# A decoder layer on one core: attention's bias stored four times side by side, and one buffer for the whole-number activations

## The chip, the core and the metric

The program runs on one core of a Trainium2 chip. A core has five engines with a queue of instructions each: TensorE (PE in the profile) multiplies matrices, with weight loads in a row of their own (PEld); VectorE (DVE), ScalarE (ACT) and GpSimd (POOL) work element by element; SyncE (SP) issues DMAs, and ScalarE issues some, too. Each engine takes its instructions in the order of its queue and waits on semaphores for the others. The metric is the device time in microseconds (us) of one execution: 830.32 us is the median of six runs, 827.81 to 832.29.

## The reference, cut to what matters

Input x is (4, 512, 512) in fp32, and a context of (4, 512, 256). Three blocks follow each other, each with a residual and a layer norm behind it:

```python
x = _layernorm(x + attn(x))                # windows of 128 tokens, 16 heads of 16, a table of relative positions
x = _layernorm(x + ssm(ctx_1024, z=x))     # conv, softplus, a scan over 512 steps with 16 states, times silu(x)
x = _layernorm(x + ffn(x))                 # activations quantized to whole numbers, weights by their signs
```

The change touches two places of it. In attention, each window and head has scores of 128 x 128, to which one and the same bias of 128 x 128 is added before the softmax:

```python
scores = jnp.einsum('bwhqd,bwhkd->bwhqk', q, k) * scale
scores = scores + rel_bias[rel]            # rel_bias[rel]: 128 x 128, the same for all heads
```

In the last block the activations are rounded to whole numbers between -128 and 127, with one scale for each token:

```python
s = 127.0 / jnp.max(jnp.abs(x), axis=-1, keepdims=True)
xq = jnp.clip(jnp.round(s * x), -128, 127) / s
```

## The kernel before

**The work.** There are four batches (b = 0 to 3), each of 512 tokens in four windows. For each batch there are these threads of work: `ssm_inputs` (projection, convolution, step sizes), `ssm_steps` (the scan, in 4 quarters q of the channels and 4 groups n of the states), `attn_qk` and four `attn_window` (attention), `ssm_gate` (norm, gate, norm and quantization of the batch), and at the end `ffn` in two halves of 256 tokens a batch, eight halves h in all. `ffn_signs` reads the weights of the last block in the first 200 us, takes their signs on ScalarE (L718) and writes them to DRAM (L719).

**The scan.** For each state tile POOL multiplies du by a broadcast row (L390), ScalarE makes the decay by an exponential (L394), VectorE scans (L396), VectorE or POOL multiplies by a second row (L398, L400), and TensorE sums into y (L404). The two broadcast rows, bc0 and bc1, are loaded by SyncE for each n (L353). The tile of y, times the gate z (L433), is transposed (L436) and added to the residual (L438).

**The bias.** `attn_biases` loads the 128 x 128 bias once and splits it (L539 to L545) into a high part in fp32r, by a cast on ScalarE, and a low part, the rest, by VectorE. The same function splits a row of other biases, whose parts go by DMA into `rows` (L550). In `attn_window`, `scores(g)` takes four heads at a time: a PSUM bank of 128 x 512 gets the bias by two matmuls with the identity (L625), and the queries times the keys on top (L634). That is 4 batches x 4 windows x 4 groups x 2 parts, 128 matmuls. Their moving operand is a view that repeats the 128 columns four times.

**The whole numbers.** In the last part of `ssm_gate`, four tiles t of 128 tokens are scaled and rounded to v (L462), transposed on TensorE (L465), brought back by ScalarE as whole numbers in bf16 to `qT` (L468), and written to DRAM by a DMA that ScalarE issues (L469). `qT` has two buffers. Then the scales of the batch's tokens are transposed (L472), copied to `ir` (L474), and written to DRAM by SyncE (L475). The halves of the last block read both back (L759, L762). There, for each f2 of eight, `gates` multiplies 16 times for g (L778) and VectorE scales (L786), `gated` does the same for u (L802, L811), ScalarE casts the product to a high part hi (L821), POOL takes the rest lo (L823), and `down` multiplies both by the third weights (L830).

**What sets the order.** The threads are woven in Python (`weave`, L885): each has a start time, and what it yields says how far its time advances; this gives every instruction a priority. A planner of the library then places the instructions of each engine one after the other, by priority and by the times of its own model, as soon as their inputs and buffers are free in that model. So a change of a size or of a number of buffers can move instructions that it does not touch. Tiles come from pools; tiles of one tag share its buffers, and a tile that reuses a buffer waits until all readers of the one before, a DMA among them, are done. The tag "part" has two buffers, which xd (L294) and v (L461) share; the tag "state" has four, which the scan's tiles share with the row of biases and its two parts.

Of the kernel before, what the change touches and what calls it, by code (L numbers as in the profile page):

```python
# [10 lines left out]
F32 = mybir.dt.float32  # L11
F32R = mybir.dt.float32r
BF16 = mybir.dt.bfloat16
# [5 lines left out]
P = 128  # L19
# [3 lines left out]
NT = S // P  # L23
NC = H // P
# [38 lines left out]
BP = 2  # L63
# [17 lines left out]
def decoder_layer_kernel(  # L81
# [24 lines left out]
    small = ctx.enter_context(tc.tile_pool(name="small", bufs=4, side="left"))  # L106
# [3 lines left out]
    def bank(name):  # L110
        return psum.tile([P, 512], F32, tag="mm", name=name)

    def ssm_bank(name):
        return psum.tile([P, 512], F32, tag="aux", name=name, bufs=BX)
# [25 lines left out]
    def moments(v, eps, what, home):  # L140

        with tc.high_priority(HP):
            return moments_(v, eps, what, home)
# [37 lines left out]
    def silu(dst, src, back=True):  # L181

        f = nc.scalar.activation(dst, src, AF.Silu)
        if not back:
            return
        with tc.issue_after(f.ins), tc.high_priority(10 * HP):
            nc.scalar.preload_act_table_set("natural_log_exp_and_others")

    def normalize(dst, src, rs, nb, i, func=AF.Identity):
        nc.scalar.activation(dst, src, func, scale=rs[:, i : i + 1], bias=nb[:, i : i + 1])  # L190
# [3 lines left out]
    mp = ctx.enter_context(tc.tile_pool(name="mp", bufs=2, side="right"))  # L194
# [24 lines left out]
    for j in range(NQ):  # L219
# [6 lines left out]
            rhs=col[:, C_AL : C_AL + NE * DS],  # L226
# [188 lines left out]
    def ssm_gate(b):  # L415
        acc = mp.tile([P, NT, DI], F32, tag="acc", name=f"acc{b}", bufs=1)
        for w in range(NT):
            nc.sync.dma_start(out=acc[:, w, :], in_=x0d[b][:, w, :])
        _, rs, nb = moments(acc, 1e-5, f"a{b}", lambda: ssm_bank(f"root_ps{b}"))
        for w in range(NT):  # L420
            normalize(acc[:, w, :], acc[:, w, :], rs, nb, w)

        z = mp.tile([P, NE, S], F32, tag="z", name=f"z{b}", bufs=1)
        silu(z, acc)
        for q in range(NE):
            while f"y{b}{q}" not in done:
                yield 1
            y = ssm_y[b, q]
            if (b, q) in LATE:
                y = mp.tile([P, S], F32, tag="yr", name=f"yr{b}_{q}", bufs=BR)  # L430
                nc.sync.dma_start(out=y, in_=yd[b, q])
            with tc.high_priority(HP):
                nc.vector.tensor_tensor(z[:, q, :], z[:, q, :], y, ALU.mult)  # L433
            pt = ssm_bank(f"yT_ps{b}_{q}")
            for t in range(NT):
                nc.tensor.transpose(pt[:, ts(t, P)], z[:, q, ts(t, P)], ident)  # L436
            to = acc[:, :, ts(q, P)]
            nc.vector.tensor_tensor(to, to, pt.rearrange("p (t e) -> p t e", e=P), ALU.add)  # L438
        yield 4
        mv, rs, nb = moments(acc, 1e-5, f"m{b}", lambda: pt)  # L440
        amax = small.tile([P, NT], F32, tag="amax", name=f"amax{b}", bufs=1)
        for t in range(NT):
            normalize(acc[:, t, :], acc[:, t, :], rs, nb, t)
            nc.vector.tensor_reduce(amax[:, t : t + 1], acc[:, t, :], AX.X, ALU.max, apply_absolute_value=True)
        nc.scalar.dma_start(out=x2d[b], in_=acc)
        yield 4


        s = small.tile([P, NT], F32, tag="s", name=f"s{b}", bufs=1)
        nc.vector.reciprocal(s, amax)  # L450
        nc.vector.tensor_scalar_mul(s, s, 127.0)
        v2 = small.tile([P, NT], F32, tag="v2", name=f"v2{b}", bufs=1)
        nc.gpsimd.tensor_tensor(v2, mv[:, :, 1], rs, ALU.mult)
        nc.gpsimd.tensor_tensor(v2, v2, rs, ALU.mult)
        r2 = rsqrt(v2, 1e-8, NT, f"f{b}")
        iv = inv_s[:, b * NT : (b + 1) * NT]
        nc.gpsimd.tensor_scalar_mul(iv, amax, 1 / 127.0)
        nc.gpsimd.tensor_tensor(iv, iv, r2, ALU.mult)
        yield 4
        for t in range(NT):  # L460
            v = mp.tile([P, H], F32, tag="part", name=f"v{b}_{t}", bufs=BP)  # L461
            nc.scalar.activation(v, acc[:, t, :], AF.Identity, scale=s[:, t : t + 1], bias=consts[ROUND])  # L462
            pt = ssm_bank(f"qT_ps{b}_{t}")
            for c in range(NC):
                nc.tensor.transpose(pt[:, ts(c, P)], v[:, ts(c, P)], ident)  # L465

            qT = mp.tile([P, NC, P], BF16, tag="qT", name=f"qT{b}_{t}", bufs=2)
            nc.scalar.activation(qT.rearrange("p c t -> p (c t)"), pt, AF.Identity, bias=consts[-ROUND])  # L468
            nc.scalar.dma_start(out=qd[b][:, :, ts(t, P)], in_=qT)  # L469
            yield 2  # L470
        pt = ssm_bank(f"is_ps{b}")
        nc.tensor.transpose(pt[:NT, :P], iv, ident)  # L472
        ir = small.tile([NT, P], F32, tag="ir", name=f"ir{b}", bufs=1)
        nc.scalar.copy(ir, pt[:NT, :P])  # L474
        nc.sync.dma_start(out=isd[b], in_=ir)  # L475

# [35 lines left out]
    def attn_biases(aw, ap, aq, ws):  # L512

        ws["v"] = aw.tile([P, NM, NR, NM, 32], F32, tag="wv", name="wv_s")
        ws["d"] = aw.tile([P, NM, H], F32, tag="wd", name="wd_s")
        for c in range(NM):
            for m in range(NM):
                nc.sync.dma_start(
                    out=ws["v"][:, c, :, m, :], in_=wv[ts(c, P), ts(m, P)].rearrange("p (r k) -> p r k", k=32)
                )  # L520
        ws["v"] = ws["v"].rearrange("p c r m k -> p c (r m k)")
        for r in range(NR):
            for m in range(NM):
                c, p0 = divmod((r * NM + m) * 32, P)
                nc.sync.dma_start(out=ws["d"][p0 : p0 + 32, c, :], in_=wd[m * P + r * 32 : m * P + r * 32 + 32, :])
        raw = ap.tile([P, P], F32, tag="at", name="bias")
        nc.sync.dma_start(out=raw, in_=relb)
        row = mp.tile([1, HC + H], F32, tag="state", name="row", bufs=BS)
        for m in range(NM):
            nc.sync.dma_start(  # L530
                out=row[:, :HC].rearrange("o (r m k) -> o m r k", m=NM, k=32)[:, m],
                in_=rows[:, ts(m, P)].rearrange("o (r k) -> o r k", k=32),
            )
        nc.sync.dma_start(out=row[:, HC:], in_=rows[:, HC:])


        def split(v, name, pool, tags):

            bufs = BS if pool is mp else 1  # L539
            hi = pool.tile(list(v.shape), F32R, tag=tags[0], name=f"{name}_hi", bufs=bufs)  # L540
            lo = pool.tile(list(v.shape), F32R, tag=tags[1], name=f"{name}_lo", bufs=bufs)
            with tc.issue_after(ssm_exp[0].ins):
                nc.scalar.copy(hi, v)
            nc.vector.tensor_tensor(lo, v, hi.bitcast(F32), ALU.subtract)
            return hi, lo  # L545

        ws["bias"] = split(raw, "bias", aw, ("bias_hi", "bias_lo"))
        ws["row"] = aw.tile([2, HC + H], F32R, tag="rows", name="rows")
        for i, part in enumerate(split(row, "row", mp, ("state", "state"))):
            nc.sync.dma_start(out=ws["row"][i : i + 1, :].bitcast(F32), in_=part.bitcast(F32))  # L550
        yield 1
# [51 lines left out]
    def attn_window(b, w, aw, ap, aq, ws):  # L603
        n = f"{b}_{w}"
        tok = ts(w, P)
        cT, qT, kT = attn_x[b]
# [15 lines left out]
        def scores(g):  # L622
            psc = bank(f"sc_ps{n}_{g}")
            for i in range(2):
                nc.tensor.matmul(  # L625
                    psc,
                    lhsT=ws["ident"],
                    rhs=ws["bias"][i].unsqueeze(1).to_broadcast([P, 4, P]),
                    start=(i == 0),
                    stop=False,  # L630
                )
            rows_ = ts(g, 32)
            for m in range(NM):
                nc.tensor.matmul(  # L634
                    psc[:, ts(m, 2 * P)],
                    lhsT=qT[rows_, m, tok],
                    rhs=kT[rows_, m, :, tok],
                    start=False,
                    stop=(m == NM - 1),
                    tile_position=(32 * g, 0),  # L640
                )
            nc.vector.tensor_reduce(  # L642
                ntop[:, 4 * g : 4 * g + 4], psc.rearrange("p (h k) -> p h k", k=P), AX.X, ALU.max, negate=True
            )
            pscs[g] = psc

        scores(0)
        yield 1
        pa = None
        for g in range(NG4):  # L650
# [17 lines left out]
            for j in range(4):  # L668
# [3 lines left out]
                    rhs=scT[:, j, :],  # L672
# [324 lines left out]
```

## Time and profile before

| What | Value |
|---|---|
| Median of six runs | 830.32 us (827.81 to 832.29) |
| The profiled execution's own time | 830.23 us |
| Its span, first to last instruction | 828.4 us |
| Mean granted clock of TensorE | 0.956 |
| Busy share PE, DVE, ACT, POOL | 91%, 78%, 71%, 67% |
| L625, high part: count, mean of one | 64, 527 ns |
| L625, low part: count, mean of one | 64, 400 ns |
| L468 (qT): count, mean of one | 16, 679 ns |
| L469 (its DMA): median to landing | 3.0 us |
| L543, cast of the bias, 128 x 128 | 298 ns |
| L544, its low part, 128 x 128 | 281 ns |

The profile is of one execution. Busy time is the time in which an engine executed something. In the slices each digit is the busy share of one fortieth of the span (20.7 us), in tenths. The chain is followed back from the last instruction, at each step to what released it. In lists of instructions in order of time the columns are the start in us, the duration in us, the engine, the line, the operation, the tiles (out<-in, without numbers) and the count; brackets hold the idle time of the engine ahead of it and what ended it. SPq and ACTq are the issue of DMAs from these engines' queues.

### The profile page before, as it was taken

How to read it: one execution, taken by the hardware profiler on the slowest of the kernel's cores; microseconds unless marked ns; L12 is line 12 of the kernel's file. 1: busy time of each engine (PE TensorE's matmuls, PEld its weight loads, DVE VectorE, ACT ScalarE, POOL GpSimd, SP SyncE). 2: the span in 40 equal slices, each digit the busy share in tenths (PEclk: the TensorE clock that was granted, in tenths of full speed). 3: DMA queues.
4: the chain of work that ended last, by engine and by line, in shares of the span. 5: the costliest groups of instructions: out<-in, count | busy, mean ns of one | idle time of the engine just before them, and what ended most of it. 6: DMA issues, size and time to landing. Idle time of an engine off the chain costs nothing.

```text
span 828.4 us, 11702 instructions
## 1 busy us (share of the span) xinstructions
PE 755.2 (91%) x3906; PEld 411.4 (50%) x3906; DVE 649.6 (78%) x943; ACT 590.9 (71%) x1038; POOL 556.6 (67%) x323
## 2 busy tenths in 40 slices
PE   9978899999899999899988998798788999999995
PEld 4323344444344444344434454356464667777773
DVE  5359586898999887989989699979998978453542
ACT  4558789787775976877797877696595777845551
POOL 2157489688678779787865977786989844233342
PEclk9897999999899999999999999989999999999998
DMA  7887789966342437564334285671334112301100
GB/s 213 292 275 215 231 266 323 314 214 216 89 139 100 151 87 262 195 219 150 112 105 131 87 281 198 195 299 47 128 115 139 52 40 102 92 24 51 52 26 26
DMA packets 82784, 129.49 MB, mean 156 GB/s; under 512 B 18690, under 2 KB 29074, under 8 KB 81444
## 3 DMA queue, kind: packets, MB, share of 16 engines
q1 hardware_dynamic: 65844, 108.77, 40.1%
q10 hardware_dynamic: 16880, 19.98, 7.0%
q8 instruction: 31, 0.51, 0.2%
q14 instruction: 29, 0.24, 0.1%
HBM read 91.48 MB, written 37.23 MB: 155 GB/s over the span
## 4 chain that ended last, share of the span: by engine, by line
PE 53%; DVE 21%; ACT 12%; DMA 7%; issue 5%; SPq 1%; POOL 1%; ACTq 0%; DVEq 0%; POOLq 0%
PE d_ps L830 11%; DVE da L396 5%; PE y L404 5%; PE u_ps L802 4%; PE g_ps L778 4%; PE sc_ps L634 4%; DVE state L396 4%; DMA sgd<-sgn_sgd 3%; PE c_ps L568 3%; PE sc_ps L625 2%; PE a_ps L701 2%; ACT da L394 2%; DVE state L398 2%; PE in_ps L273 2%; PE xd_ps L297 2%
## 5 line engine op out<-in xcount | busy, mean ns | idle before, releaser
L390 POOL TENSOR_TENSOR state<-du,bc 128x1024 f32<-128x1024 f32 x128 | 301.7, 2371 | 110.2 <-PE y L404 67.6
L394 ACT ACTIVATE da<-d,a_neg 128x512 f32<-128x512 f32 x256 | 175.1, 697 | 63.4 <-DVE state L398 39.4
L400 POOL TENSOR_TENSOR state<-state,bc 128x1024 f32<-128x1024 f32 x64 | 151.7, 2370 | 38.4 <-DVE state L396 25.0
L396 DVE TENSOR_TENSOR_SCAN state<-da,state 128x512 f32<-128x512 f32 x128 | 152.5, 1208 | 27.7 <-ACT da L394 21.9
L396 DVE TENSOR_TENSOR_SCAN da<-da,state 128x512 f32<-128x512 f32 x128 | 152.9, 1214 | 14.9 <-ACT da L394 14.9
L823 POOL TENSOR_TENSOR lo<-gs,hi 128x512 fp32r<-128x512 f32 x64 | 81.9, 1282 | 107.3 <-ACT hi L821 88.2
L404 PE MATMUL y<-state,sel 128*32 128x512 f32 x512 | 101.5, 641 | 7.6 <-DVE state L398 4.9
L398 DVE TENSOR_TENSOR state<-da,bc 128x512 f32<-128x512 f32 x128 | 84.7, 678 | 0.8
L658 ACT ACTIVATE sc<-sc_ps,ntop 128x128 f32<-128x128 f32 x256 | 73.9, 376 | 12.0 <-DVE ntop L642 11.2
L821 ACT CAST hi<-gs 128x512 fp32r<-128x512 f32 x64 | 39.2, 616 | 59.5 <-DVE gs L811 44.0
L830 PE MATMUL d_ps<-sd,hi 128*128 128x512 f32 x256 | 74.8, 412 | 4.6 <-DVE nb_a L164 2.0
L830 PE MATMUL d_ps<-sd,lo 128*128 128x512 f32 x256 | 76.5, 421 | 0.0
L802 PE MATMUL u_ps<-taken,su 128*128 128x256 bf16 x512 | 67.6, 273 | 8.0 <-DVE gs L811 5.8
L634 PE MATMUL sc_ps<-k,q 32*128 32x256 f32 x256 | 73.8, 411 | 1.0 <-ACT q L590 1.0
L778 PE MATMUL g_ps<-taken,sg 128*128 128x256 bf16 x512 | 68.8, 279 | 4.5 <-DVE gs L811 3.2
L811 DVE TENSOR_TENSOR gs<-gs,u_ps 128x512 f32<-128x512 f32 x64 | 43.4, 680 | 34.9 <-PE u_ps L802 34.9
L786 DVE TENSOR_TENSOR gs<-g_ps,taken 128x512 f32<-128x512 f32 x64 | 43.4, 683 | 33.9 <-PE g_ps L778 30.4
L802 PEld LDWEIGHTS <-su 128*128 128x128 fp8e4 x512 | 46.2, 98 | 32.4 <-issue 24.9
L778 PEld LDWEIGHTS <-sg 128*128 128x128 fp8e4 x512 | 47.5, 100 | 29.1 <-issue 23.0
L634 PEld LDWEIGHTS sc_ps<-k,q 32*128 32x128 f32 x256 | 42.4, 187 | 30.7 <-issue 23.8
L642 DVE TENSOR_REDUCE ntop<-sc_ps 128x4 f32<-128x512 f32 x64 | 43.3, 677 | 14.7 <-PE sc_ps L634 14.5
L830 PEld LDWEIGHTS d_ps<-sd,hi 128*128 128x128 f32 x256 | 45.7, 191 | 17.2 <-DVE nb_a L164 2.8
(161 smaller groups left out, 1185.2 us busy)
## 6 DMA issues: line engine op xcount, KB each, us to landing
d<-dd SPq DMA_DIRECT2D x60, 256.0 KB, 3.9
du<-dud SPq DMA_DIRECT2D x60, 256.0 KB, 4.5
bc<-bcd SPq DMA_DIRECT2D x32, 256.0 KB, 4.1
xT<-in_xT_dram SPq DMA_DIRECT2D x16, 256.0 KB, 4.7
xa<-in_x_dram SPq DMA_DIRECT2D x16, 256.0 KB, 3.5
raw_sgd<-in_wgT_dram SPq DMA_DIRECT2D x16, 256.0 KB, 4.3
ud<-u ACTq DMA_DIRECT2D x4, 1024.0 KB, 4.3
uq<-ud SPq DMA_DIRECT2D x16, 256.0 KB, 2.9
```

What stands on the lines that cost most here:

```text
L390: nc.gpsimd.tensor_tensor(st, du, bb.unsqueeze(1).to_broadcast([P, 2, S]), ALU.mult)
L394: nc.scalar.activation(da, d[:, j, :], AF.Exp, scale=a_neg[:, a : a + 1])
L396: nc.vector.tensor_tensor_scan(to, da, st[:, j, :], 0.0, ALU.mult, ALU.add)
L398: nc.vector.tensor_tensor(st[:, j, :], da, cb, ALU.mult)
L400: nc.gpsimd.tensor_tensor(st, st, cb.unsqueeze(1).to_broadcast([P, 2, S]), ALU.mult)
L404: nc.tensor.matmul(y[ts(j, EB), :], lhsT=sel, rhs=sts[j], start=False, stop=(n == NG - 1), tile_position=(0, EB * j))
L634: nc.tensor.matmul(psc[:, ts(m, 2 * P)], lhsT=qT[rows_, m, tok], rhs=kT[rows_, m, :, tok], start=False, stop=(m == NM - 1), tile_position= ...
L658: nc.scalar.activation(sc[:, j, :], psc[:, ts(j, P)], AF.Exp, bias=ntop[:, h : h + 1])
L778: nc.tensor.matmul(pg[:, ts(j, HS)], lhsT=sg[:, c, ts(2 * f2 + j, P)], rhs=qT[:, c, :], start=(c == 0), stop=(c == NC - 1),)
L802: nc.tensor.matmul(pu[:, ts(j, HS)], lhsT=su[:, c, ts(2 * f2 + j, P)], rhs=qT[:, c, :], start=(c == 0), stop=(c == NC - 1),)
L823: nc.gpsimd.tensor_tensor(lo, g2, hi.bitcast(F32), ALU.subtract)
L830: nc.tensor.matmul(pos[t], lhsT=part[:, j, ts(t, P)], rhs=sd[:, 2 * f2 + j, :], start=(f2 + j == 0 and part is parts[0]), stop=(f2 == NF2 ...
```

## The change

The bias is split from a view that repeats it four times, so its two parts are stored as 128 x 4 x 128, and the matmuls read them as they lie. Each part takes 2 KB in each partition instead of 0.5 KB. The cast and the subtraction are done on 512 columns instead of 128, once. To `qT` the change gives one buffer instead of two (1 KB less in each partition), and `ir` no longer has a buffer of its own: it takes one of the two of the tag "part" (0.5 KB less).

```diff
-            qT = mp.tile([P, NC, P], BF16, tag="qT", name=f"qT{b}_{t}", bufs=2)
+            qT = mp.tile([P, NC, P], BF16, tag="qT", name=f"qT{b}_{t}", bufs=1)
             nc.scalar.activation(qT.rearrange("p c t -> p (c t)"), pt, AF.Identity, bias=consts[-ROUND])
             nc.scalar.dma_start(out=qd[b][:, :, ts(t, P)], in_=qT)
             yield 2
         pt = ssm_bank(f"is_ps{b}")
         nc.tensor.transpose(pt[:NT, :P], iv, ident)
-        ir = small.tile([NT, P], F32, tag="ir", name=f"ir{b}", bufs=1)
+        ir = mp.tile([NT, P], F32, tag="part", name=f"ir{b}", bufs=BP)
...
-        ws["bias"] = split(raw, "bias", aw, ("bias_hi", "bias_lo"))
+
+        ws["bias"] = split(raw.unsqueeze(1).to_broadcast([P, 4, P]), "bias", aw, ("bias_hi", "bias_lo"))
...
                     lhsT=ws["ident"],
-                    rhs=ws["bias"][i].unsqueeze(1).to_broadcast([P, 4, P]),
+                    rhs=ws["bias"][i],
```

The changed kernel has one line more, so that its lines from 546 on are one higher.

## The prediction

> **What bounds the kernel now.** I read the busy rows and the slices of the page first, then a table by stage, then who waits for whom on TensorE.
>
> ```profile
> PE 755.2 (91%) x3906; PEld 411.4 (50%) x3906; DVE 649.6 (78%) x943; ACT 590.9 (71%) x1038; POOL 556.6 (67%) x323
> PE   9978899999899999899988998798788999999995
> PE 53%; DVE 21%; ACT 12%; DMA 7%; issue 5%; SPq 1%; POOL 1%; ACTq 0%; DVEq 0%; POOLq 0%
> ```
>
> TensorE carries the kernel: 91% of the span and 53% of the chain that ended last. The dips in its row lie near the start and between slices 24 and 31. By stage (columns: stretch in us, its length, then busy us with the count of instructions of PE, weight loads, DVE, ACT, POOL, the granted clock, the DMA share and GB/s):
>
> ```profile
> 0.00:60.00 60.00, 52.78 (x115) 21.60 (x117) 27.71 (x47) 29.36 (x46) 17.79 (x25) 0.91 0.81 257
> 560.00:620.00 60.00, 50.75 (x324) 35.18 (x323) 59.39 (x91) 42.29 (x61) 48.72 (x30) 0.97 0.27 93
> 680.00:720.00 40.00, 38.74 (x268) 30.67 (x266) 29.15 (x64) 27.79 (x41) 13.48 (x19) 1.00 0.28 93
> ```
>
> From 560 to 620 VectorE is the bound (59.39 of 60 us) and TensorE waits for it; from 680 on TensorE is the bound. The waits on TensorE between 560 and 640 (us in total, times, longest) say the same, and add up to 12.5 us; from 640 to the end the same view adds up to 2.4 us:
>
> ```profile
> PE u_ps L802 <- DVE gs L811: 3.1, 3, 1.7
> PE y L404 <- DVE state L398: 2.5, 2, 2.4
> PE g_ps L778 <- DVE gs L811: 2.1, 3, 0.9
> PE d_ps L830 <- DVE gs L786: 1.8, 1, 1.8
> ```
>
> So after 640 every microsecond by which TensorE's next input is late lies on the path. The profiled execution took 830.23 us (span 828.4), the median of the runs is 830.32; I sum against 830.23.
>
> **The change part by part.**
>
> *The bias matmuls: 0.* 128 of them read 512 columns, through a view now, side by side then. One pair (start, length):
>
> ```profile
> 256.95 0.50 PE L625 MATMUL sc_ps<-bias_hi,identr 128*128 128x512 f32 x1
> 257.28 0.39 PE L625 MATMUL sc_ps<-bias_lo,identr 128*128 128x512 f32 x1
> 257.51 1.88 PE L273 MATMUL in_ps<-hT,in_s 128*128 128x512 f32 x4
> ```
>
> From the second to the matmul behind it pass 0.23 us. The matmuls of L830 have the same type and width, read contiguous memory, and stand 16 in 3.66 us on the chain (669.63), 0.23 each. The view costs nothing that could be saved. Bounds: 128 x 0.01 us of rounding, -1.3 to 0.
>
> *The split: 0.* bias_hi grows from 0.30 us (the row at 128x128) to about 0.62 (the cast of 128x512 at L821), bias_lo from 0.28 to about 0.68 (the 128x512 tensor op at L398). ScalarE next waits 1.43 us for TensorE (the copy at 35.81), VectorE 2.74 us (the copy at 37.65): both cover it. Without cover, +0.3 and +0.4.
>
> *SyncE's queue: +0.5.* In the built program of the changed kernel the order of queued work is the same on every engine up to the last third, but for the first 60 us: two DMAs (the second weight row bc1 of n=2, and row_lo) stand ahead of the first write of signs, and on ScalarE the two copies of d (L336) come ahead of two exponentials (L394).
>
> ```profile
> 43.34 0.53 SPq L719 DMA_DIRECT2D sgd<-sgn_sgd  x1
> 47.91 1.15 ACT L718 ACTIVATE sgn_sgd<-raw_sgd 128x512 fp8e4<-128x512 f32 x2 [9.55 <-DMA sgd<-sgn_sgd]
> 49.56 0.69 ACT L394 ACTIVATE da<-d,a_neg 128x512 f32<-128x512 f32 x1
> ```
>
> ScalarE stands 9.55 us for that write to land, with the exponentials queued behind and VectorE's scans behind these. Two issues of 0.55 to 0.6 us make it 1.2 late, the swapped copy (0.57) makes the first exponential 1.75 late. But at 53.16 ScalarE waits again (0.97 us) for the third write of signs, which slips only from 49.33 to about 49.8, because the number of DMAs ahead of it is unchanged. Bounds 0 and +1.75; +0.5 is what passes the second wait.
>
> *One qT buffer: +2.5.* Each qT (L468, ScalarE) now waits until the DMA of the one before has landed. Landing:
>
> ```profile
> DMA to landing us min/median/max: 2.2/3.0/5.8
> ```
>
> Batches 0 and 1 keep their order. There only the fourth tile is late: at 370.26 the DMA issued at 364.90 lands at 370.71 (+0.45; the next row on ScalarE waits 0.63 for VectorE), and at 527.89 one lands at 528.59 (+0.7; the next waits 1.59). Covered: 0.
>
> Batch 3 (before: qT at 709.30, 711.17, 714.31, 717.44). A DMA issues some 0.1 us after the instruction ahead of it on ScalarE has started (710.01 against 709.88). The new order is qT0, v2, table load, silu, table load, DMA0, hi2_0_0, qT1, v3, DMA1, hi2_0_1, nt_o, qT2, root, DMA2, two normalizations, qT3. Between DMA0's issue and qT1 lie 1.2 + 0.6 us, so 1.2 of the 3.0 are left as a stall; between DMA1 and qT2 0.5 + 0.6 + 0.3, 1.6 left; between DMA2 and qT3 0.1 + 1.5, 1.4 left: 4.2 us. Up to hi2_0_2 ScalarE had idled 1.36 and 0.51 there:
>
> ```profile
> 714.31 0.69 ACT L468 ACTIVATE qT<-qT_ps,const 128x512 bf16<-128x512 f32 x1 [1.36 <-PE qT_ps L465]
> 716.91 0.62 ACT L821 CAST hi<-gs 128x512 fp32r<-128x512 f32 x1 [0.51 <-DVE gs L811]
> ```
>
> 2.3 remain. Queued behind are hi2_0_1 and hi2_0_2, on which POOL's lo and TensorE's down matmuls wait; TensorE took hi2_0_2 at 718.03, 0.5 after its end, so 1.8 us fall on a TensorE that has no idle time left. With landings of 2.2 nothing remains; of 5.8, about 10.
>
> Batch 2 (before: 614.67 to 627.91): by the same count 1.2 and 1.6 us of stall, with exponentials for VectorE's scans behind. VectorE has gs products to do meanwhile and ScalarE is busy 42 of 60 us; bounds 0 and 2.8, I take 0.7, nearer the covered end.
>
> [...]
>
> *ir in the ring of part: 0.* It is written at 375.6, 533.3, 670.3 and 720.2; the next tiles that could want its slot (xd at 451, v at 509, 611 and 707) come at least 37 us later, twelve times a landing. An early reuse would cost one landing, 3.0.
>
> *The order after 530: 0, bounds -7 and +4.6.* The planner puts batch 2's gate earlier (VectorE's moments by up to 17 places, TensorE's transpose of inv_s by 144) and the state steps of batch 3 later (VectorE up to 17 places, TensorE's y matmuls 40 to 76). At one place in VectorE's queue, up to five state steps are fewer and as many small moments more, and the products gs at most two more; at 650 us both queues have done the same. VectorE was saturated, so nothing is gained or lost by order alone unless a gap closes or opens on TensorE: the ends are the second and third rival.
>
> Sum: 0 + 0 + 0.5 + 1.8 + 0.7 + 0 = +3.0; 830.23 + 3.0 = 833.2 us.
>
> **The rivals.**
>
> *Hidden anyway: 830.7.* Only the early 0.5 is left. For it: ScalarE is busy 27.79 of 40 us around batch 3's gate, and landings there were 3.0 and 2.2. Against: the stalls stand in a queue that feeds TensorE where it has no slack.
>
> *Faster: 826.2.* The gaps of 12.5 us between 560 and 640 close, because y matmuls that waited for states (2.36 us at 632.51) stand later and down matmuls ahead of them. If 7 go, 833.2 - 7. It decides (over 0.3% faster) from 5.5. Against: VectorE is at 59.39 of 60 there, and most gaps wait for its products.
>
> *Slower still: 837.8.* TensorE runs in order, and the transposes of batch 3's first v now stand 60 places (703.9 instead of 708.5) earlier; before, v3_0 ended at 708.1, 0.4 ahead of them. If the gate comes no earlier, TensorE stands 4.6 us: 833.2 + 4.6. For it: the state steps ahead of that gate moved back. Against: its moments and z products moved forward, too.
>
> **How the numbers follow.** Chances: the forecast 0.34 (831 to 836), hidden 0.22, faster 0.23, slower still 0.21. About 0.3% (2.5 us) is what a measurement of this kernel can tell from no change. Slower than 832.8: 0.27 of the forecast and all of 0.21, 0.48. Within: 0.07 of the forecast, 0.20 of hidden, 0.01 of faster, 0.28. Faster: 0.22 and 0.02 of hidden, 0.24. The range runs from the faster case to somewhat past the slower one, since long landings reach further: 826 to 840.
>
> **What would show it.** Right: L625's mean within 10 ns of now; the wait at L718 near 48 us about 1 us longer; at L468 ScalarE waits for DMAs of 1 to 2 us each in batches 2 and 3, and TensorE waits at L830 for hi of batch 2 that sum to about 2 us after 700. Wrong: if L625 drops to half; if waits for qT's DMAs are absent; if TensorE's waits between 560 and 640 sum to under 7 us, or one of over 3 us stands before L465 of batch 3.

## The result, and the profile after

The changed kernel takes 838.84 us (median of 33 runs), the kernel before 832.29 us (median of the 75 runs beside them). The ratio is 1.0083, with a 95% interval of 1.0063 to 1.0103: some 7 us slower. The forecast was 833.2 us with a range of 826 to 840. In a later comparison on one chip the changed kernel took 836.58 us against 831.85, a ratio of 1.0061 (1.0031 to 1.0091). Some executions of these kernels are some per cent longer at a lower granted clock (the kernel before beside e12: 862.12 us at 0.914, another 831.24 at 0.953): ratios and intervals go by the others alone, while the medians are of all, and the traces of the runs e1, e2 and e4 below are of such longer executions.

The profiled execution took 835.18 us, its span is 833.4. The page's busy row, the slices of TensorE with its clock, and the shares of the chain by engine:

```profile
PE 759.0 (91%) x3906; PEld 414.9 (50%) x3906; DVE 646.9 (78%) x943; ACT 590.7 (71%) x1038; POOL 557.9 (67%) x323
PE   9988899999899999899988998698897989999995
PEclk9888999999899999999999999999998989999998
PE 49%; DVE 18%; ACT 15%; DMA 8%; issue 5%; POOL 2%; SPq 1%; ACTq 0%; DVEq 0%; POOLq 0%
```

No engine has more work to do, since the instruction counts are equal; TensorE is busy 759.0 us where it was 755.2. In TensorE's row the slice from 667 to 688 us (the 33rd) has an 8 where before had a 9, and an 8 in the clock's row below it where before had a 9. The stages, as before:

```profile
0.00:60.00 60.00, 53.88 (x111) 22.43 (x112) 28.33 (x47) 29.95 (x46) 16.76 (x25) 0.89 0.81 261
560.00:620.00 60.00, 52.21 (x329) 35.71 (x328) 57.14 (x91) 42.17 (x60) 47.61 (x30) 0.97 0.34 113
680.00:720.00 40.00, 39.11 (x245) 28.61 (x244) 25.04 (x60) 24.51 (x37) 13.13 (x18) 0.99 0.18 63
```

From 560 to 620 TensorE does slightly more than before (52.21 against 50.75). The waits on TensorE between 560 and 640 still add up to 12.1 us; from 640 to the end they are 5.9 us where they were 2.4:

```profile
PE yT_ps L436 <- DVE acc L438: 3.9, 2, 2.9
PE d_ps L831 <- ACT hi L822: 1.0, 2, 0.7
PE g_ps L779 <- DVE gs L812: 0.8, 1, 0.8
PE u_ps L803 <- DVE gs L812: 0.2, 1, 0.2
```

The first line is new in this stretch: transposes of batch 3's gate, `yT` (L436). I lay a window of 40 us over the place in every trace, from 130 us behind the end of batch 1's last qT transposes. It is counted from there because the granted clock in the stages up to there differed from one trace to the next even where the order of work is the same (from 200 to 350 us it was 0.94 before, 0.94 after and 0.89 in e1), so it is not the change that moves it. Before, that is 658 to 698 us:

```profile
658.00:698.00 40.00, 39.07 (x246) 28.18 (x245) 32.09 (x64) 27.09 (x34) 19.05 (x16) 1.00 0.15 47
```

and after, 657 to 697:

```profile
657.00:697.00 40.00, 35.77 (x211) 25.14 (x208) 30.69 (x53) 24.75 (x29) 18.27 (x11) 0.91 0.14 44
```

TensorE stands 4.2 us of the 40 instead of 0.9, and while it is busy it runs at 0.91 of its clock instead of 1.00, which by this estimate is worth another 35.77 x 0.09 = 3.2 us. I call the sum of the two the loss: 0.93 us before, 7.45 after, a difference of 6.5. From the end of batch 1's last qT transposes to the end of the last down matmul the two traces take 290.9 us (527.9 to 818.7) and 297.0 (526.6 to 823.6). So the window holds the whole difference of 6.1, and a little is won back elsewhere. The place, on TensorE:

```profile
667.82 1.05 PE L803 MATMUL u_ps<-taken,su 128*128 128x256 bf16 x8
668.70 0.60 PE L436 MATMUL yT_ps<-ident,z 128*128 128x128 f32 x4
669.23 1.06 PE L404 MATMUL y<-state,sel 128*32 128x512 f32 x8
673.16 0.66 PE L436 MATMUL yT_ps<-ident,z 128*128 128x128 f32 x4 [2.86 <-DVE acc L438]
674.87 1.11 PE L436 MATMUL yT_ps<-ident,z 128*128 128x128 f32 x4 [1.05 <-DVE acc L438]
675.64 2.06 PE L831 MATMUL d_ps<-sd,lo 128*128 128x512 f32 x4
677.49 2.76 PE L831 MATMUL d_ps<-sd,hi 128*128 128x512 f32 x6
```

TensorE stands 2.86 us ahead of the transposes of yT3_1 and 1.05 ahead of those of yT3_2, since each needs the one bank that VectorE's `acc` (L438) still has to read. Then ten down matmuls take 0.44 us each (675.64 to 680.05) instead of 0.23: the granted clock is 1.00 up to 673.5 and 0.50 from 674.0 to 680.0. VectorE, at the same place:

```profile
665.24 1.28 DVE L433 TENSOR_TENSOR z<-z,yr 128x512 f32<-128x512 f32 x2
666.45 0.68 DVE L398 TENSOR_TENSOR state<-da,bc 128x512 f32<-128x512 f32 x1
670.06 0.69 DVE L433 TENSOR_TENSOR z<-z,yr 128x512 f32<-128x512 f32 x1 [2.93 <-DMA yr<-yd]
670.67 0.68 DVE L812 TENSOR_TENSOR gs<-gs,u_ps 128x512 f32<-128x512 f32 x1
671.30 1.22 DVE L396 TENSOR_TENSOR_SCAN state<-da,state 128x512 f32<-128x512 f32 x1
672.44 0.66 DVE L438 TENSOR_TENSOR acc<-acc,yT_ps 128x512 f32<-128x512 f32 x1
```

Behind the first two z products it waits 2.93 us for a reload, yr3_2, which SyncE could issue (665.96) only when the first z product had freed one of the two yr buffers; then come a product, a scan and `acc`. And ScalarE:

```profile
660.83 1.28 ACT L183 ACT_TABLE_LOAD   x1
662.13 1.92 ACT L183 ACTIVATE z<-acc 128x2048 f32<-128x2048 f32 x1
664.06 1.28 ACT L187 ACT_TABLE_LOAD   x1
665.36 0.62 ACT L822 CAST hi<-gs 128x512 fp32r<-128x512 f32 x1
665.99 1.28 ACT L183 ACT_TABLE_LOAD   x1
667.28 1.91 ACT L183 ACTIVATE gs<-gs 128x2048 f32<-128x2048 f32 x1
669.21 1.28 ACT L187 ACT_TABLE_LOAD   x1
670.51 0.69 ACT L394 ACTIVATE da<-d,a_neg 128x512 f32<-128x512 f32 x1
```

The silu of batch 3's z starts at 662.13, 14.7 us earlier than before (676.84), and now stands right ahead of the silu of a gs tile; with their table loads the two fill 660.8 to 670.5 but for one cast. The exponential behind them (670.51) belongs to the scan of the last group, which stands ahead of `acc` on VectorE. So two things end here about 1 us apart, the reload (670.06) and the exponential (671.20).

In before's order the last exponential (665.07) and the last scans (667.35) were done before the silu of batch 3's z began, the third z product of a reloaded y stood later (682.66), and the transposes of yT waited for nothing:

```profile
665.07 0.69 ACT L394 ACTIVATE da<-d,a_neg 128x512 f32<-128x512 f32 x1 [0.42 <-DVE state L396]
667.07 1.91 ACT L183 ACTIVATE gs<-gs 128x2048 f32<-128x2048 f32 x1
667.35 2.34 DVE L396 TENSOR_TENSOR_SCAN da<-da,state 128x512 f32<-128x512 f32 x2
676.84 1.92 ACT L183 ACTIVATE z<-acc 128x2048 f32<-128x2048 f32 x1
678.99 1.27 DVE L433 TENSOR_TENSOR z<-z,yr 128x512 f32<-128x512 f32 x2
680.97 0.60 PE L436 MATMUL yT_ps<-ident,z 128*128 128x128 f32 x4
682.66 0.66 DVE L433 TENSOR_TENSOR z<-z,yr 128x512 f32<-128x512 f32 x1
682.98 0.60 PE L436 MATMUL yT_ps<-ident,z 128*128 128x128 f32 x4
```

### The profile page after: what moved, and what is told of

The parts are those of the page before. It is cut to its first block, busy times and chain, and to the rows that moved or that the text cites. A ratio compares the mean times of both kernels' runs of the same rounds, so it can differ in the third digit from the quotient of the medians.

```text
span 833.4 us, 11706 instructions
## 1 busy us (share of the span) xinstructions
PE 759.0 (91%) x3906; PEld 414.9 (50%) x3906; DVE 646.9 (78%) x943; ACT 590.7 (71%) x1038; POOL 557.9 (67%) x323
## 4 chain that ended last, share of the span: by engine, by line
PE 49%; DVE 18%; ACT 15%; DMA 8%; issue 5%; POOL 2%; SPq 1%; ACTq 0%; DVEq 0%; POOLq 0%
PE d_ps L831 10%; DVE da L396 5%; PE y L404 5%; PE sc_ps L635 4%; PE g_ps L779 4%; PE u_ps L803 4%; DVE state L396 4%; ACT da L394 3%; PE sc_ps L626 2%; PE c_ps L569 2%; DVE state L398 2%; PE a_ps L702 2%; DMA sgd<-sgn_sgd 2%; PE in_ps L273 2%; PE xd_ps L297 2%
## 5 line engine op out<-in xcount | busy, mean ns | idle before, releaser
L394 ACT ACTIVATE da<-d,a_neg 128x512 f32<-128x512 f32 x256 | 175.1, 696 | 65.3 <-DVE state L398 42.0
L831 PE MATMUL d_ps<-sd,hi 128*128 128x512 f32 x256 | 77.4, 423 | 10.3 <-DVE gs L787 3.5
```

The source lines that it names most:

```text
L394: nc.scalar.activation(da, d[:, j, :], AF.Exp, scale=a_neg[:, a : a + 1])
L831: nc.tensor.matmul(pos[t], lhsT=part[:, j, ts(t, P)], rhs=sd[:, 2 * f2 + j, :], start=(f2 + j == 0 and part is parts[0]), stop=(f2 == NF2 ...
```

## The experiments

All are compared with the kernel before on the same chip, and are named below by the number in front of their label. Each has one trace, of one execution, whose own time can lie some us from the median (e6: 831.79 us for 835.83). The table collects them; "loss" is TensorE's loss in the 40 us, by the rule above.

| Run | What | Ratio to before (95%) | Loss, us |
|---|---|---|---|
| | before | | 0.93 |
| | changed kernel | 1.0083 (1.0063 to 1.0103) | 7.45 |
| e11_changed_again | changed kernel, measured again | 1.0061 (1.0031 to 1.0091) | 7.71 |
| e1_only_qT1 | only qT's buffers | 1.0065 (1.0036 to 1.0093) | 7.29 |
| e4_bias_hi_wide | only the bias, high part | 1.0011 (0.9975 to 1.0048) | 0.93 |
| e2_qT1_batch3 | one qT buffer in batch 3 | 0.9984 (0.9956 to 1.0013) | 0.94 |
| e8_qT1_batch1 | one qT buffer in batch 1 | 1.0060 (1.0028 to 1.0093) | 7.45 |
| e3_yr_own_buffer | changed, reload's wait removed | 1.0120 (1.0068 to 1.0171) | 7.25 |
| e9_downs_first | changed, down matmuls first | 1.0059 (1.0018 to 1.0100) | 3.39 |
| e10_qT1_batch1_downs_first | e8, down matmuls first | 1.0034 (1.0005 to 1.0063) | 4.66 |
| e7_z_silu_late | changed, z's silu later | 1.0037 (1.0005 to 1.0069) | 4.84 |
| e6_no_silu | changed, a silu left out | 1.0041 (1.0009 to 1.0072) | 2.88 |
| e5_no_silu_own_buffer | e3 and e6 together | 1.0048 (1.0016 to 1.0080) | 4.68 |
| e12_before_no_silu | before, that silu left out | 1.0005 (0.9981 to 1.0030) | 1.44 |

### Which part of the change?

**Only qT's buffers.** The edit to the kernel before:

```diff
-            qT = mp.tile([P, NC, P], BF16, tag="qT", name=f"qT{b}_{t}", bufs=2)
+            qT = mp.tile([P, NC, P], BF16, tag="qT", name=f"qT{b}_{t}", bufs=1)
```

> The kernel before with only qT's buffers cut from two to one; bias and ir as before. Its order of work equals that of the changed kernel on every engine from 60 us on. Theory A (the new order lets batch 3's third z product stand ahead of its reload yr3_2, TensorE stands behind it and then runs at a lower clock): +6 to +8 us against before, with VectorE's wait of about 3 us at L433 for yr near 670 us. Theory B (ScalarE's waits for qT's DMAs carry the loss themselves): also +6 to +8. Theory C (the loss comes from the bias, the early queue): 0, within 1 us.

Measured 837.5 us against 832.68, 1.0065: all of the change's loss within the intervals, and the same loss of 7.29 us at the same place. Theory C falls.

**Only the bias.** The high part alone is stored four times, the low part stays a view, and qT keeps its two buffers:

```diff
+            wide = v.unsqueeze(1).to_broadcast([P, 4, P]) if pool is aw else v
-            hi = pool.tile(list(v.shape), F32R, tag=tags[0], name=f"{name}_hi", bufs=bufs)
+            hi = pool.tile(list(wide.shape), F32R, tag=tags[0], name=f"{name}_hi", bufs=bufs)
...
-                nc.scalar.copy(hi, v)
-            nc.vector.tensor_tensor(lo, v, hi.bitcast(F32), ALU.subtract)
+                nc.scalar.copy(hi, wide)
+            nc.vector.tensor_tensor(lo, v, (hi[:, 0, :] if pool is aw else hi).bitcast(F32), ALU.subtract)
...
-                    rhs=ws["bias"][i].unsqueeze(1).to_broadcast([P, 4, P]),
+                    rhs=ws["bias"][i].unsqueeze(1).to_broadcast([P, 4, P]) if i else ws["bias"][i],
```

> The kernel before with the bias's high part alone side by side four times (the low part through the view, qT with two buffers, ir as before). TensorE, VectorE and POOL keep their order; SyncE has the two DMAs ahead of the first write of signs and ScalarE the two swapped copies, as the changed kernel has. Theories A and B: 0 within 1 us (my early term: +0.5), the high part's matmuls 497 ns median as before. Theory C: +3 to +7.

Measured 832.96 us against 832.68, 1.0011: no difference. In its trace the high part's matmuls have a median of 499 ns, 498 before.

**One qT buffer in batch 3, or in batch 1, alone.** Two tags of one buffer each; a batch in the list uses the first for all its tiles (the second kernel has `(1,)`):

```diff
-            qT = mp.tile([P, NC, P], BF16, tag="qT", name=f"qT{b}_{t}", bufs=2)
+            qT = mp.tile([P, NC, P], BF16, tag="qTa" if b in (3,) or t % 2 == 0 else "qTb", name=f"qT{b}_{t}", bufs=1)
```

> The kernel before with one qT buffer in batch 3 alone (batches 0 to 2 keep two). The order is that of before up to about 710 us. Theory A: 0 to +1.5 us against before, since the reload yr3_2 keeps its late place. Theory B: +2 to +7, and my own term for this part was +1.8. Theory C: 0.

> The kernel before with one qT buffer in batch 1 alone: batches 0, 2 and 3 have two. The planner's order of the last third is that of the changed kernel, but for 37 places on TensorE around the down matmuls of batch 2's gate and 8 on VectorE. Theory A2: the order makes the loss, +5 to +8 us against before, with TensorE's wait at L436 near 673 us. Theory B (waits of batches 2 and 3): 0 to +2.

Batch 3 alone: 0.9984, no difference in the time. ScalarE's waits for qT's DMAs, in the view of that tile:

```profile
  DMA qTd<-qT: 1.7, 2
```

They can be seen in the trace: from the last down matmul of half 3 to that of half 4 it takes 33.3 us, before 31.5. So the direct price in batch 3 is 1.8 us in one trace, too little for the comparison of times.

Batch 1 alone: 1.0060, all of the loss within the intervals, with two buffers in batches 2 and 3 where I had put the cost. Its order in the last third is nearly that of the changed kernel, and its loss in the 40 us is the same 7.45. This is the result that decides between waits and order: one buffer in batch 1 costs its time 140 us later, by what the planner then does. Its one wait for a qT's DMA (2.1 us, at batch 1's fourth tile) stands ahead of the window. That it costs nothing itself is read from the traces, in which the window holds the whole difference; no run has the new order with two buffers in every batch.

### Which wait?

**The reload gets a buffer of its own.** From the changed kernel:

```diff
-                y = mp.tile([P, S], F32, tag="yr", name=f"yr{b}_{q}", bufs=BR)
+                y = mp.tile([P, S], F32, tag="yr" if (b, q) != (3, 2) else "part", name=f"yr{b}_{q}", bufs=BR)
```

> The changed kernel, but batch 3's third reload, yr3_2, takes a buffer of the tag part, idle then, instead of waiting for the buffer of yr3_0. The order is that of the changed kernel on TensorE, ScalarE and POOL; on VectorE one product stands one place earlier, on SyncE the load five places earlier. Theory A: VectorE's wait at L433 for yr and TensorE's waits at L436 near 673 us vanish, 5 to 8 us are won against the changed kernel, so -2 to +2 us against before. Theory B and C: as slow as the changed kernel, +6 to +8 against before.

This was my first theory after the result, and it fell: 1.0120, no faster than the changed kernel. The reload's wait is gone, but nothing is won. VectorE in this kernel, whose trace is 10.3 us later at this place:

```profile
675.58 2.98 DVE L433 TENSOR_TENSOR z<-z,yr 128x512 f32<-128x512 f32 x3
679.27 0.69 DVE L812 TENSOR_TENSOR gs<-gs,u_ps 128x512 f32<-128x512 f32 x1
681.64 1.23 DVE L396 TENSOR_TENSOR_SCAN state<-da,state 128x512 f32<-128x512 f32 x1 [1.69 <-ACT da L394]
682.78 0.66 DVE L438 TENSOR_TENSOR acc<-acc,yT_ps 128x512 f32<-128x512 f32 x1
```

The three z products run together, and VectorE then waits 1.69 us for the exponential behind the silus. `acc` starts where it would have started anyway, 682.78 - 10.3 = 672.5, and TensorE stands 3.6 us, 3.9 in the changed kernel:

```profile
683.50 1.12 PE L436 MATMUL yT_ps<-ident,z 128*128 128x128 f32 x4 [2.84 <-DVE acc L438]
685.39 1.12 PE L436 MATMUL yT_ps<-ident,z 128*128 128x128 f32 x4 [0.78 <-DVE acc L438]
686.16 2.06 PE L831 MATMUL d_ps<-sd,lo 128*128 128x512 f32 x4
```

**Down matmuls ahead of the transposes.** One edge of order on TensorE, with no wait in it, in the changed kernel and in the one with a single buffer in batch 1:

```diff
-            for t in range(NT):
-                nc.tensor.transpose(pt[:, ts(t, P)], z[:, q, ts(t, P)], ident)
+            with tc.issue_after(downs[2, 7].ins) if (b, q) in ((3, 1),) else ExitStack():
+                for t in range(NT):
+                    nc.tensor.transpose(pt[:, ts(t, P)], z[:, q, ts(t, P)], ident)
...
-                        nc.tensor.matmul(
+                        downs[h, f2] = nc.tensor.matmul(
```

> The changed kernel, with the transposes of yT3_1 put behind the down matmuls of half 2, f2 of 6 and 7, in TensorE's queue, with one edge of order and nothing else; these matmuls are ready at 667.7 and 671.8 us of the profiled execution, while TensorE stands from 670.3 to 673.2. Theory A3 (TensorE's own order makes the loss: it stands ahead of transposes that wait for the one bank, with ready matmuls behind them, and the clock falls afterwards): the waits at L436 near 673 us sum to under 1 us, the four and six matmuls behind run at 0.23 us each and not 0.42, and 4 to 7 us are won against the changed kernel, 0 to +3 us against before. Theory D (the gate of batch 3 itself, whichever way TensorE is filled, sets the end): as the changed kernel, +5 to +8.

> The kernel before with one qT buffer in batch 1 alone, as in the run of that name, and the same edge of order on TensorE. Theory A3: 4 to 7 us less than that run, 0 to +3 us against before; against the run with the changed kernel and the same edge, the waits of qT in batch 3 are gone, worth under 1 us. Theory D: +5 to +8 against before.

> The changed kernel as it is, beside the two others on the same chip: +5 to +9 us against before.

The time of the first is 836.46 us beside 836.58 of the changed kernel on that chip: not told apart. In the trace the waits at yT are gone and the clock stays at 1.00, so the loss falls from 7.71 to 3.39 us; but TensorE, in order, meets the next thing that hangs on ScalarE:

```profile
672.86 1.19 PE L833 MATMUL d_ps<-sd,lo 128*128 128x512 f32 x4
674.43 1.19 PE L833 MATMUL d_ps<-sd,hi 128*128 128x512 f32 x4 [0.38 <-ACT hi L824]
678.30 0.72 PE L833 MATMUL d_ps<-sd,hi 128*128 128x512 f32 x2 [2.69 <-ACT hi L824]
```

(The line numbers of this kernel are two higher from L436 on.) That cast, hi of half 3, is queued on ScalarE behind the last exponentials. And 1.5 us are given back later, where TensorE waits for batch 3's fourth qT:

```profile
PE is_ps L474 <- ACT qT L470: 1.5, 1, 1.5
```

From batch 1's last transposes to the last down matmul it is 294.7 us against 296.9: 2.2 us are won in the trace. The kernel with one buffer in batch 1 alone has no such wait in batch 3, and comes to 1.0034, where 4 to 7 us less than e8's 1.0060 had been expected; the two are not told apart, and in its trace the granted clock is at 0.96 in the window, not at 1.00. So A3 is right about the clock in one of the two traces, and wrong about the waits.

**The silu of z behind the last exponential.** From the changed kernel, where `last["e"]` is the newest exponential of L394:

```diff
-        silu(z, acc)
+        with tc.issue_after(last["e"].ins) if b == 3 else ExitStack():
+            silu(z, acc)
```

> The changed kernel, with the silu of batch 3's z put behind the last exponential of the scan on ScalarE; the planner then puts the z products and transposes behind the last scan group, as before had them. Theory A2: the stall near 673 us is gone, -3 to +2 us against before (the changed kernel was 2.8 us ahead at 640 us, and the waits of qT in batch 3 stay). Theory B: +5 to +8.

Measured 1.0037, some 3 us over before, and a loss of 4.84 us: between the two kernels, and more than A2 allowed. Now the transposes of yT3_0 wait, 3.02 us, for a z product that waits for this silu.

### Which engine?

**A silu left out.** With and without the reload's own buffer, and in the kernel before:

```diff
-            if f2 % NS2 == NS2 - 1:
+            if f2 % NS2 == NS2 - 1 and (h, f2) != (3, NF2 - 1):
                 silu(gss[-1], gss[-1])
```

> The kernel of the run with yr3_2's own buffer, and beside it the silu of one tile (half 3, f2 of 4 to 7) with its two table loads left out, 4.5 us of ScalarE that stand ahead of the exponentials of batch 3's last scan group; the output is not the reference's there. TensorE, POOL and SyncE keep their order. Theory A2 (TensorE stands ahead of the transposes of yT3_1 because the one bank is read by an acc that VectorE reaches only behind two things that end at the same time: the product that waits for the reload, and the scan that waits for an exponential behind two silus): now both are gone, TensorE's waits at L436 near 673 us sum to under 1 us, and the time is -1 to +2 us against before, 5 to 8 us less than the changed kernel. Theory B (ScalarE's waits for qT's DMAs): +5 to +8, as the changed kernel.

> The changed kernel with the same silu and its two table loads left out, yr3_2 in its shared buffer as there (the output is not the reference's in that tile). TensorE, POOL and SyncE keep their order. Theory A2: the reload still stands in the way, TensorE's waits at L436 near 673 us remain at 2.5 to 4 us, +4 to +8 us against before. If it is 4.5 us of ScalarE's work as such that counts: as fast as the run that leaves out the silu and has the own buffer.

> The kernel before, with the same silu of one tile and its two table loads left out as in the runs above (its output is not the reference's there). On TensorE 8 instructions change their place. Theory S (in the changed kernel's order this silu stands right behind z's, 9.1 us of ScalarE in one piece ahead of the last exponentials; in the order of before the two are 10 us apart and it costs nothing): within 0.3% of before, and the stretch from batch 1's last qT transposes to the end within 2 us of the 290.9 of before, where the changed kernel went from 297.0 to 290.8. Theory E (4.5 us of ScalarE's work there are worth 3 to 6 us in any order): 3 to 6 us less than before, in the time and in that stretch.

In the kernel before it is worth nothing in the time (1.0005); in the trace the stretch to the last down matmul is 288.1 us for 290.9, 0.8 more than Theory S allowed, but other traces in before's order differ as much (289.1 in e2, 292.0 in e4). In the changed one the loss in the window falls from 7.45 to 2.88, and the time is at 1.0041:

```profile
659.00:699.00 40.00, 37.12 (x235) 25.95 (x233) 33.38 (x62) 23.51 (x33) 18.74 (x14) 1.00 0.13 44
```

So it is not ScalarE's work as such that makes most of it; it is where this silu stands in the new order. But A2's figures failed: I expected nothing without the own buffer and 5 to 8 us with it. Without it the reload comes in time by itself, since VectorE's scans go ahead of the product (it waits 0.27 us for it, not 2.93). And in both kernels TensorE still stands ahead of yT, 2.3 and 2.8 us, because VectorE does the scans ahead of `acc`.

**What follows.** The five traces with the new order on TensorE and ScalarE as the planner made it (after, e1, e3, e8, e11) lose 7.25 to 7.71 us in the 40, the four with the order of before there (before, e2, e4, e12) 0.93 to 1.44. From batch 1's last transposes to the last down matmul the five take 294.5 to 297.3 us, the four 288.1 to 292.0. That the loss comes with the order, and the order with qT's buffer, is shown. What the order does wrong is not one wait: batch 3's gate begins 15 us earlier, ahead of the last scan group, and three engines in order then hang on each other. Each wait that was taken away was followed by another of 1.5 to 3 us; what went was part of the standing and, in e6 and e9, all of the loss by the clock. The times of the five kernels in between (e5, e6, e7, e9, e10: 1.0034 to 1.0059) lie between those of the two orders, but all are slower than before, and their intervals overlap or touch that of the changed kernel, so that they gain is read from the traces (290.8 to 294.7 us in that stretch) and not shown by the times. Which single edit of the order would bring back all of it stays open, and no version here is shown to be faster than the kernel before.

## Why the prediction came out as it did

The time lies in the forecast's range, but not for the forecast's reasons. Of its +3.0 us, +1.8 were to be waits for qT in batch 3 and +0.5 SyncE's queue, and neither shows in the times (0.9984 in e2, 1.0011 in e4); the waits of batch 2, +0.7, did not come. The loss came from the term that stood at 0, the order. That the range still held it is in part luck: its upper end was set for long landings and a gap of 4.6 us at another place.

**The bias matmuls, 0: right.** Their rows after:

```profile
L626 PE MATMUL sc_ps<-bias_hi,identr x64: 473/497/799, 61.9 to 499.3; 128*128 128x512 f32 x64
L626 PE MATMUL sc_ps<-bias_lo,identr x64: 387/397/398, 62.3 to 499.6; 128*128 128x512 f32 x64
```

Medians of 497 and 397 ns, 498 and 397 before. What was told of the view holds: it cost nothing, so there was nothing to win.

**The split, 0: right; SyncE's queue, +0.5: nothing.** The wait at L718 ends at 48.64 instead of 47.91, and the next ones take the delay up: the signs taken at 58.41 before are taken at 58.24 after. The sign "about 1 us longer" showed as 0.7 us later; the wait itself is 9.48 us for 9.55. The run with the bias alone (e4) has this part too and is at 1.0011.

**One qT buffer, +2.5.** Batches 0 and 1, 0: right for the waits. The fourth tiles wait 1.93 and 3.08 us for their DMAs; before, ScalarE had waited 1.57 and 1.28 there for TensorE. So they come some 0.4 and 1.8 us later, where 0.45 and 0.7 had been worked out: in batch 1 the DMA ahead landed 3.9 us after its issue, and not 2.8. No wait of TensorE for these tiles shows in the trace. Batch 3, +1.8: the run with batch 3 alone gives 1.8 in its trace, but by 1.7 us of waits and not by 4.2 less what is covered, so that the figure agrees by luck; in the changed kernel it is one wait of 0.90. Batch 2, +0.7: no wait; its tiles stand 3 to 9 us apart. So the sign "waits of 1 to 2 us each in batches 2 and 3" failed, and so did that of 2 us of TensorE waiting for hi behind 700 us: it waits 1.0 there.

**ir in the ring of part, 0.** Not run by itself. With this part alone the built program has the same order as before on every engine, and e1, without it, has the loss.

**The order after 530, 0 with ends of -7 and +4.6: this is the step that failed.** I wrote that VectorE was saturated, so order alone gives nothing unless a gap closes or opens on TensorE, and looked for the gap in two places: the 12.5 us between 560 and 640, which stayed (12.1), and the transposes of v3_0 (L465) around 704, which do not wait. The gap opened between the two, at 673, at other transposes of the same gate (L436), and its price was 6.5 us in the window and not 4.6 at most, since I priced only the standing: TensorE stands 3.3 us more than before there, and the clock takes another 3.2 by the estimate above. The ground for it could have been seen: in the built program of the changed kernel ScalarE's queue has z's silu next to the gs silu, and the last scan group's exponentials behind them.

**The rivals.** "Hidden anyway" is right about the waits and wrong about the sum. "Faster" failed: the gaps between 560 and 640 did not close (12.1 of 12.5 us). "Slower still", 837.8, came nearest to the time: its mechanism, in-order TensorE standing ahead of transposes of batch 3's gate that moved forward, is the one seen, 30 us earlier and at another line than it named. A wait of over 3 us ahead of L465, its own sign, did not come.

## What to carry to other kernels

Where a planner sets the order, as here, a smaller buffer had two prices: the waits for it (1.7 us in batch 3 in e2's trace), and what the planner does with it everywhere behind. The second was the larger, 6.5 us in the window, and 140 us away; each part of the change can be built alone and its order compared engine by engine before the waits are costed. And where several in-order engines met, the wait that the profile names was only the last of several that ended close together (the reload at 670.06, the exponential at 671.20): measure what the busy engine loses over the whole place, standing and clock, and believe a cause only when taking it away brings that back.

## What the runs showed of the hardware

At the place near 673 us the granted clock fell in some traces and not in others. The table has the lengths for which TensorE stood there, in order, with the four transposes of yT in between where there were any; the time of what ran next; and the mean granted clock of the 40 us.

| Trace | TensorE stands, us | What ran next | Clock |
|---|---|---|---|
| after | 2.86, four transposes in 0.66, 1.05 | four transposes in 1.11, four down matmuls in 2.06 | 0.91 |
| e3 | 2.84 | four transposes in 1.12, and behind another 0.78 four more in 1.12 | 0.91 |
| e5 | 2.01, four transposes in 0.66, 0.78 | four transposes in 1.12, four down matmuls in 2.06 | 0.96 |
| e7 | 3.02 | four transposes in 0.86 | 0.96 |
| e10 | 2.57 | two down matmuls in 0.85, the next four in 1.91 | 0.96 |
| e6 | 1.53, four transposes in 0.66, 0.78 | four transposes in 0.66, four down matmuls in 1.17 | 1.00 |
| e9 | 2.69 | two down matmuls in 0.72, the next four in 1.09 | 1.00 |

How long TensorE stands before the clock falls was not to be read from one number: with no transposes in between it fell behind 2.57 us of standing (e10) and not behind 2.69 (e9). The ends of matmuls are modelled in the profile, so the lengths are good to some tenths, and these two can't be told apart. What decides whether the clock falls is not shown by these runs.
